# A grouped 3x3 convolution on one core: which images are computed by which of three schemes, and from where on a step is issued one image earlier

## The chip, the cores and the metric

The kernel runs on one core of a Trainium2 chip. The metric is the time of one execution on the device in microseconds; a kernel's time is the median of several executions. The engines are TensorE (PE, with its weight loads as PEld), VectorE (DVE), ScalarE (ACT), GpSimd (POOL) and SyncE (SP).

## What is computed

Input x has 160 images of 128 channels by 32x32 in float32. Each is normalised by groups of four channels (mean and variance over the group and all pixels), convolved 3x3 with padding 1, and the result is added to x. The weights come from U, five sets of 128x128x9, quantised in two steps. In memory the images of one set are five apart; the kernel takes all 32 images of set 0 first, then set 1, and so on.

```python
w = (v1 + v2).reshape(OUT_CH * N, IN_CH, K, K)          # v1, v2: U floored to steps s1, s2
act = conv_general_dilated(x.reshape(B // N, N * C, H, W), w, padding=1, feature_group_count=N)
x = x + act                                             # the convolution's input is _gn(x)
```

## The kernel before, in words

**Numbers.** The matmuls are in fp16. A normalised image is split into a high part hi (fp16 of it) and a low part lo (what is left, fp16 again), and both go through the convolution. An image's result lies in two PSUM banks, even and odd (of rows, or of columns), of 512 columns each.

**Two schemes.** The direct way to fill a bank is nine taps: one matmul for each of the nine weights, on the rows that this parity of output needs (`taps`, L771, matmul L784). The cheaper way goes through four combinations of neighbouring rows or columns with summed weights, three matmuls for each combination (`product`, L819, matmul L839). Combination 2 with the weights SUM is put into the even bank (`begin`, L847); a copy of that bank, half, is taken by ACT (`leave`, L902, copy L907); combination 3 with the weights DIFF goes on top (`complete`, L854); and DVE makes the odd bank as 2 x half - even (`odd_from_even`, L909, L914). Then the combinations 0 and 1 are added, one for each bank, in two passes (`main`, L892).

- A *by-rows* image uses taps for hi and combinations for lo. DVE makes lo (L747) and then the combinations, called rows, in three operations (L760, L768, L769). POOL makes the normalised z (L710), or ACT does for the first image of a statistics group (L636); ACT makes hi from it (L644).
- A *combined* image (`combined`, L647) uses combinations for both parts. The combinations v are made of the input itself: POOL makes part (L674, L704), DVE the rest (L686, L693). ACT scales them to vh (L734) and DVE makes vl (L740).
- Images 0 to 2 use taps for both parts (`direct_hi`, `direct_lo`).

Images 7 to 29 are combined where odd, 30 to 129 where i%5 is 0, 2 or 4, and the rest where i%4 is not 2.

**Order of work.** Each engine executes its queue in the order in which `run` (L993) issues it; nothing is reordered. Iteration i of its loop (L1125) issues `conv(i)` (L863) for PE, and around it the steps of images further on: the low part of image i+2 (i+3 after 13, both 15 and 16 at 13, by `step_of`, L983), the high part one further, v or z two further. On ACT an iteration has, in order: half, the sums over images to be measured (L241), the copies of the finished banks of image i-1 (L942), hi or vh, the squares of the images measured (L248), and columns of weights for the next set (`keep_taps`, L564). On DVE: the low part, the combine steps, odd of image i+1, then v (L686, L693), small statistics steps (L296 and following), and the measuring of a few images (L231, `BY_VECTOR`). Between them DVE gets one or two steps of the quantising of the next set's weights (`later.take`; L142 to L162). POOL's v, z and rstd wait for the last but one low-part instruction of DVE (L1207, `after`).

`conv(i)` has two forms. Before image `TWO_AHEAD` (28) it issues begin(i+1), main(i, 0), leave(i+1), complete(i+1), main(i, 1): half is awaited one pass later. From 28 on it issues complete(i+1), begin(i+2), main(i, 0), main(i, 1), and leave(i+2) follows among ACT's later steps, so half has a whole image's time.

**Buffers.** lo has four (image number modulo four), even four banks, odd three, rows and vl five together, hi and vh four each. POOL's accumulating DMA adds each result to an output that already holds the input (L963).

Of the kernel before, what the change touches and what calls it, by code (L numbers as in the profile page):

```python
# [36 lines left out]
class Later:  # L37
# [25 lines left out]
    def finish(self):  # L63
        run(self.steps)
# [110 lines left out]
def last_of(steps, last=None):  # L175
    for last in steps:
        pass
    return last


def run(steps):

    while True:
        try:
            next(steps)
        except StopIteration as end:
            return end.value
# [134 lines left out]
def general_path(tc, keep, steps, x, u, out):  # L322
# [8 lines left out]
    with tc.If(far > 0), ExitStack() as ctx:  # L331
# [9 lines left out]
        for n in range(N_SETS):  # L341
            un = one.tile([P, C, TAPS], F32, tag="u", name=f"g_u{n}")
            nc.sync.dma_start(un, uv[n])
            wn = one.tile([P, C, TAPS], F32, tag="w", name=f"g_w{n}")
            k1, k2 = run(steps.quantise(one, un, f"g{n}", F32))
            nc.vector.tensor_scalar_mul(wn, k1, steps.s1)
            nc.vector.scalar_tensor_tensor(wn, k2, steps.s2, wn, ALU.mult, ALU.add)
# [38 lines left out]
class Main:  # L386
# [23 lines left out]

    STAT_LEAD = 15
    FURTHER = 11
    TWO_AHEAD = 28
    LOAD_LEAD = 18
    CHUNKS = 11
    STEADY = 7
    BY_VECTOR = (8, 10, 11, 14, 19, 24, 29, 34)
    FIFTHS = 30
    THIRDS = 130
# [171 lines left out]
    def keep_sums(self, n, col):  # L591
        wt = self.wts[n, col]
        run(self.both_sums(
            self.nc.gpsimd, wt[:, self.SUM], wt[:, self.DIFF], *(wt[:, k] for k in range(ROW))
        ))
# [6 lines left out]
    def by_vector(self, i):  # L602
        return i in self.BY_VECTOR

# [42 lines left out]
    def combined(self, i):  # L647

        if i < self.STEADY or i >= self.imgs:
            return False  # L650

        if i < self.FIFTHS:
            return i % 2 == 1
        return i % 5 % 2 == 0 if i < self.THIRDS else i % 4 != 2

    def by_scalar_too(self, i):

# [113 lines left out]
    def taps(self, i, part, col, target, parities=(0, 1)):  # L771


        nc, H, W = self.nc, self.H, self.W
        tile, top = part
        n, _ = self.place(i)
        dw = col - 1
        c0, c1 = max(0, -dw), W - max(0, dw)
        for k in self.KS:
            for a in parities:  # L780

                first, end = int(a + k == 0), H // 2 - int(a + k == 3)
                s0 = 2 * first + a + k - 1 + top
                nc.tensor.matmul(  # L784
                    target[a][:, first:end, c0:c1],
                    self.wts[n, col][:, k, :],
                    tile[:, s0 : s0 + 2 * (end - first) - 1 : 2, c0 + dw : c1 + dw],
                    start=(i < self.FIRST and col == self.COLS[0] and k == 1 and top == 0),
                    stop=False,
                    skip_group_check=True,  # L790
                )
# [54 lines left out]

    def begin(self, i):  # L847

        even = self.bank_of(self.ps_even, i)
        self.eo[i] = [even]  # L850
        for step in self.KS:
            self.product(even, i, 2, step, self.SUM, start=step == self.KS[0])

    def complete(self, i):  # L854

        for step in self.KS:
            self.product(self.eo[i][0], i, 3, step, self.DIFF)

    def steady(self, i):

        return i >= self.TWO_AHEAD

    def conv(self, i, on_the_way):  # L863


        ahead = range(i + 1, self.imgs)[:1]
        if self.steady(i) and self.steady(i - 1):
            for k in ahead:
                self.complete(k)
            for k in range(i + 2, self.imgs)[:1]:  # L870
                self.begin(k)
            self.main(i, 0, lambda: on_the_way(self.COLS[1]))
            self.main(i, 1, lambda: on_the_way(self.COLS[2]))
        elif i == self.FIRST:
            self.main(i, 0)
            self.begin(i + 1)
            on_the_way(self.COLS[1])
            self.main(i, 1)
            on_the_way(self.COLS[2])
            self.leave(i + 1)  # L880
            self.complete(i + 1)
        else:
            self.begin(i + 1)
            self.main(i, 0, lambda: on_the_way(self.COLS[1]))
            self.leave(i + 1)
            self.complete(i + 1)
            if self.steady(i):
                self.begin(i + 2)
            self.main(i, 1, lambda: on_the_way(self.COLS[2]))
        del self.v[i]  # L890

    def main(self, i, a, between=lambda: None):  # L892

        to = self.eo[i][a]
        for step in self.KS:
            if step == self.KS[1] and a == 1 or step == self.KS[2] and a == 0:
                between()
            if not self.combined(i):
                self.taps(i, (self.hi[i], 0), step, self.eo[i], (a,))
            self.product(to, i, a, step, 2 * a)  # L900

    def leave(self, i):  # L902

        half = self.half[i] = self.evac.tile(
            [self.P, self.H // 2, self.W], F32, tag="half", name=f"half{i}"
        )
        self.nc.scalar.copy(half, self.eo[i][0])  # L907

    def odd_from_even(self, i):  # L909


        even, odd = self.eo[i][0], self.bank_of(self.ps_odd, i)
        self.eo[i].append(odd)
        self.nc.vector.scalar_tensor_tensor(  # L914
            odd, self.half.pop(i), 2.0, even, ALU.mult, ALU.subtract
        )
# [76 lines left out]
    def run(self):  # L993
# [54 lines left out]
        def measure(stage, *images):  # L1048
            for i in images:
                self.measure(i, (stage,))  # L1050
# [74 lines left out]
        for i in range(self.imgs):  # L1125
# [53 lines left out]
            if i < self.FIRST:  # L1179

                if i == 0:
                    measure(0, 8, 9, 10)
                if i == 1:
                    self.normalise(4)
                    self.high_part(4)
                if i == 2:
                    self.normalise(5)
                    measure(1, 9)
                    self.high_part(5)
                    self.odd_from_even(3)  # L1190
                    self.low_part(4)
                    run(self.combinations(4))
                    measure(0, 11)
                self.residual(j)
            else:

                last = None
                for k in self.step_of(i, 2):
                    if self.combined(k):
                        last = last_of(self.low_combined(k), last)  # L1200
                    else:
                        self.low_part(k)
                        later.take(1)
                        last = last_of(self.combinations(k), last)
                last = later.take(1, last)
                if last:
                    before = self.last_but_one(last)  # L1207
                    for st in scaled:
                        self.after(st.power(), before)
                    for k in self.step_of(i, 4):  # L1210
                        self.beside_pairs(k, before)
                if i > self.FIRST and self.by_hand(j):
                    self.residual(j)
                for k in by_scalar:
                    self.measure(k, (0,))
                if self.steady(i) and i + 2 < self.imgs:
                    self.leave(i + 2)
                if i > self.FIRST and not self.by_hand(j):
                    self.residual(j)
                    self.accumulate(j)  # L1220
                for st in ready:
                    if not st.late:
                        st.deviations()
                for k in self.step_of(i, 3):
                    if self.combined(k):
                        self.high_combined(k)
                        continue
                    if self.by_scalar_too(k):
                        self.normalise(k)
                    self.high_part(k)  # L1230
                for k in by_scalar:
                    self.measure(k, (1,))
# [95 lines left out]
```

## Time and profile before

| | us |
|---|---|
| median of 3 runs | 972.56 (971.38 to 973.38) |
| the profiled execution, its own time | 971.98 |
| its span, first to last instruction | 970.2 |
| mean granted TensorE clock | 0.993 of full |

The profile is of one execution. PE's busy time counts a matmul until its modelled end (0.37 to 0.38 us for 512 columns), while successive matmuls start 0.21 us apart, so a PE that is shown busy is one that never waits long. A bracket at the end of a timeline row gives the idle time of the engine ahead of it and what ended that. The granted clock is the share of full speed at which the array was let run.

| operation | engine, line | mean us |
|---|---|---|
| vl | DVE L740 | 2.50 |
| v, two parts | DVE L686, L693 | 1.66, 0.74 |
| lo; rows, three parts | DVE L747; L760, L768, L769 | 1.22; 0.69, 0.42, 0.42 |
| odd | DVE L914 | 0.69 |
| vh; hi; half | ACT L734; L644; L907 | 2.02; 1.07; 0.58 |
| z by POOL; by ACT | L710; L636 | 1.87; 1.27 |

### The profile page before, as it was taken

What the parts mean: (1) busy time and instruction counts of PE and PEld (TensorE: products, weight loads), DVE (VectorE), ACT (ScalarE), POOL (GpSimd) and SP (SyncE); (2) the same over time, 40 slices, a digit from 0 to 9 for tenths busy, and PEclk for the clock granted to TensorE, in tenths of its full rate; (3) what the DMA queues carried; (4) which work ended last, traced back from release to release, by engine and by line L of the source; (5) the groups of instructions that cost most, each with busy time, mean ns of one, the idle gap of its engine ahead of it and who ended that gap; (6) DMA issues with size and microseconds to landing.
All of it is one profiled execution on the core that took longest, in us unless ns stands there. A gap on an engine that the chain in (4) does not pass through costs nothing.

```text
span 970.2 us, 12948 instructions
## 1 busy us (share of the span) xinstructions
PE 928.3 (96%) x4432; PEld 434.6 (45%) x4432; DVE 858.9 (89%) x1125; ACT 863.3 (89%) x1320; POOL 446.0 (46%) x481
## 2 busy tenths in 40 slices
PE   2899979999999999999999999999999999999996
PEld 1444434444444444444444444444444444444442
DVE  7988878888899899998999899898989988889973
ACT  5779879998999999999999999999999999997660
POOL 4354433544453443454445444545444455454640
PEclk9999989999999999999999999999999999999998
DMA  9079999999999999999999999999999999756554
GB/s 353 29 270 351 329 353 330 328 326 329 321 314 317 259 283 294 276 284 269 290 252 308 286 282 284 289 277 297 263 274 266 290 280 258 162 90 102 95 93 128
DMA packets 67450, 254.23 MB, mean 262 GB/s; under 512 B 5296, under 2 KB 5296, under 8 KB 67376
## 3 DMA queue, kind: packets, MB, share of 16 engines
q1 hardware_dynamic: 45344, 173.09, 47.8%
q0 software_dynamic: 22032, 80.23, 44.1%
q8 instruction: 37, 0.61, 0.2%
q14 instruction: 37, 0.30, 0.1%
HBM read 89.19 MB, written 164.10 MB: 261 GB/s over the span
## 4 chain that ended last, share of the span: by engine, by line
PE 79%; ACT 10%; DVE 5%; issue 3%; DMA 2%; POOL 1%; SPq 0%; DVEq 0%; ACTq 0%; POOLq 0%
PE even L839 43%; PE odd L839 14%; PE even L784 11%; PE odd L784 11%; ACT junk L248 2%; ACT vh L734 2%; ACT sum L942 2%; ACT junk L241 2%; DMA u<-in_L_conv_U_dram 2%; ACT z L636 1%; ACT half L907 1%; ACT hi L644 1%; DVE ext L508 1%; DVE ext L509 1%; DVE lo L747 1%
## 5 line engine op out<-in xcount | busy, mean ns | idle before, releaser
L839 PEld LDWEIGHTS <-wt 128*128 128x128 f16 x1884 | 184.3, 99 | 211.2 <-issue 4.4
L740 DVE SCALAR_TENSOR_TENSOR vl<-v,rstd,vh 128x2048 f16<-128x2048 f32 x94 | 235.2, 2502 | 48.6 <-ACT vh L734 48.4
L839 PE MATMUL even<-vh,across 128*128 128x512 f16 x564 | 211.3, 375 | 3.5 <-ACT half L907 3.5
L839 PE MATMUL even<-vl,across 128*128 128x512 f16 x564 | 211.3, 375 | 1.7 <-DVE vl L740 1.7
L734 ACT ACTIVATE vh<-v,rstd 128x2048 f16<-128x2048 f32 x94 | 190.2, 2024 | 0.0
L784 PEld LDWEIGHTS <-wt 128*128 128x128 f16 x1242 | 121.7, 100 | 144.2 <-issue 6.6
L248 ACT ACTIVATE junk<-xt,mv 128x1024 uint8<-128x1024 f32 x152 | 176.4, 1160 | 0.3
L839 PE MATMUL even<-rows,wt 128*128 128x512 f16 x567 | 174.2, 381 | 2.5 <-ACT half L907 2.4
L963 POOL DMA_DIRECT2D out_dram<-sum x153 | 135.2, 884 | 89.7 <-ACT sum L942 74.5
L241 ACT ACTIVATE junk<-xt 128x1024 uint8<-128x1024 f32 x152 | 161.2, 1060 | 12.7 <-DMA xt<-in_x_dram 9.8
L839 PEld LDWEIGHTS <-across 128*128 128x128 f16 x1128 | 110.4, 98 | 135.5 <-issue 7.5
L784 PE MATMUL even<-hi,wt 128*128 128x496 f16 (+3 forms) x594 | 162.9, 379 | 4.8 <-DVE odd L914 3.8
L710 POOL TENSOR_SCALAR z<-xt,ngm,rstd 128x1024 f32<-128x1024 f32 x49 | 91.8, 1873 | 152.1 <-DVE rows L769 50.5
L784 PE MATMUL odd<-hi,wt 128*128 128x496 f16 (+3 forms) x594 | 161.0, 375 | 0.0
L686 DVE TENSOR_TENSOR v<-xt 128x960 f32<-128x960 f32 x94 | 155.8, 1658 | 0.5 <-POOL v L674 0.5
L907 ACT COPY half<-even 128x512 f32<-128x512 f32 x157 | 90.6, 577 | 60.1 <-PE even L839 57.1
L674 POOL TENSOR_SCALAR v<-xt,ngm 128x64 f32<-128x64 f32 x94 | 59.0, 628 | 172.8 <-DVE vl L740 74.8
L914 DVE SCALAR_TENSOR_TENSOR odd<-half,even 128x512 f32<-128x512 f32 x157 | 107.8, 687 | 17.3 <-PE even L839 13.8
L839 PE MATMUL even<-vh,wt 128*128 128x496 f16 (+1 forms) x282 | 105.6, 375 | 0.0
L839 PE MATMUL even<-vl,wt 128*128 128x496 f16 (+1 forms) x282 | 105.6, 375 | 0.0
L839 PE MATMUL odd<-vl,wt 128*128 128x496 f16 (+1 forms) x282 | 105.6, 374 | 0.0
L839 PE MATMUL odd<-vh,wt 128*128 128x496 f16 (+1 forms) x282 | 105.6, 374 | 0.0
(148 smaller groups left out, 1131.1 us busy)
## 6 DMA issues: line engine op xcount, KB each, us to landing
xt<-in_x_dram SPq DMA_DIRECT2D x78, 1024.0 KB, 9.6
out_dram<-sum POOLq DMA_DIRECT2D x153, 512.0 KB, 8.8
out_dram<-xt SPq DMA_DIRECT2D x76, 1024.0 KB, 14.2
out_dram<-xt SPq DMA_DIRECT2D x7, 512.0 KB, 6.1
u<-in_L_conv_U_dram SPq DMA_DIRECT2D x4, 576.0 KB, 14.7
xt<-in_x_dram SPq DMA_DIRECT2D x4, 512.0 KB, 9.8
range<-in_L_conv_U_dram SPq DMA_DIRECT2D x3, 576.0 KB, 8.0
u<-in_L_conv_U_dram SPq DMA_DIRECT2D x2, 288.0 KB, 3.0
```

What stands on the lines that cost most here:

```text
L241: self.nc.scalar.activation(junk, image, ACTF.Copy, scale=-1.0 / image.shape[1], accum_out=self.mv[:, j, 0:1],)
L248: self.nc.scalar.activation(junk, image, ACTF.Square, bias=self.mv[:, j, 0:1], accum_out=self.mv[:, j, 1:2],)
L674: return self.nc.gpsimd.tensor_scalar(self.view(self.v[i], 0, (512 + W // 2 - 1, 2), (W // 2, H)), self.view(self.image(i), 1, (W - 3, 2), ...
L686: nc.vector.tensor_tensor(self.view(v, 1, (511, 2), (half, H), (1, half - 1)), self.view(x, 1, (1, 2), (W, H), (2, half - 1)), self.view(x ...
L710: ins = nc.gpsimd.tensor_scalar(z, self.image(i), st.ngm[:, j], st.rstd[:, j], ALU.add, ALU.mult)
L734: self.nc.scalar.mul(vh, self.v[i], st.rstd[:, j])
L740: yield self.nc.vector.scalar_tensor_tensor(vl, self.v[i], st.rstd[:, j], self.hi[i], ALU.mult, ALU.subtract)
L784: nc.tensor.matmul(target[a][:, first:end, c0:c1], self.wts[n, col][:, k, :], tile[:, s0 : s0 + 2 * (end - first) - 1 : 2, c0 + dw : c1 + dw],
L839: self.nc.tensor.matmul(out, weights, moving, start=start and j == 0, stop=False, skip_group_check=True)
L907: self.nc.scalar.copy(half, self.eo[i][0])
L914: self.nc.vector.scalar_tensor_tensor(odd, self.half.pop(i), 2.0, even, ALU.mult, ALU.subtract)
L963: added = self.nc.gpsimd.dma_start(self.ov[n, :, b], self.sum.pop(i), accum_op=ALU.add)
```

## The change

Three things change.

1. `combined`: for images 30 to 129, three of five become five of eight (i*5%8 < 5), which makes 62 of 100 combined instead of 60, and other ones. All images that start a statistics group from 32 on are now combined.
2. Images 12 and 16, so far by rows, are *plain*: taps for lo as well as for hi, into both banks. They have no rows, no begin, half, complete or odd_from_even; `main` takes both banks when it starts its first pass.
3. `TWO_AHEAD` goes from 28 to 20: the second form of `conv` starts eight images earlier.

```diff
-    TWO_AHEAD = 28
+    TWO_AHEAD = 20
...
+    PLAIN = (12, 16)
...
-        return i % 5 % 2 == 0 if i < self.THIRDS else i % 4 != 2
+        return i * 5 % 8 < 5 if i < self.THIRDS else i % 4 != 2
+
+    def plain(self, i):
+        return i in self.PLAIN
...
-                    start=(i < self.FIRST and col == self.COLS[0] and k == 1 and top == 0),
+                    start=((i < self.FIRST or self.plain(i)) and col == self.COLS[0] and k == 1 and top == 0),
...
     def begin(self, i):
 
+        if self.plain(i):
+            return
...
     def complete(self, i):
 
+        if self.plain(i):
+            return
...
-        del self.v[i]
+        self.v.pop(i, None)
 
     def main(self, i, a, between=lambda: None):
 
+        if self.plain(i) and a == 0:
+            self.eo[i] = [self.bank_of(pool, i) for pool in (self.ps_even, self.ps_odd)]
         to = self.eo[i][a]
         for step in self.KS:
             if step == self.KS[1] and a == 1 or step == self.KS[2] and a == 0:
                 between()
             if not self.combined(i):
                 self.taps(i, (self.hi[i], 0), step, self.eo[i], (a,))
-            self.product(to, i, a, step, 2 * a)
+            if self.plain(i):
+                self.taps(i, (self.los[i % len(self.los)], 1), step, self.eo[i], (a,))
+            else:
+                self.product(to, i, a, step, 2 * a)
 
     def leave(self, i):
 
+        if self.plain(i):
+            return
...
     def odd_from_even(self, i):
 
 
+        if self.plain(i):
+            return
...
-                        last = last_of(self.combinations(k), last)
+                        if not self.plain(k):
+                            last = last_of(self.combinations(k), last)
```

## The prediction

> **What bounds the kernel now.** I first read the page's busy shares, then the table of windows, which shows by stage who is full, and then the timeline of the stage that isn't.
>
> ```profile
> span 970.2 us, 12948 instructions
> ...
> PE 928.3 (96%) x4432; PEld 434.6 (45%) x4432; DVE 858.9 (89%) x1125; ACT 863.3 (89%) x1320; POOL 446.0 (46%) x481
> ```
>
> The columns below are stage, its length, busy us of PE, PEld, DVE, ACT and POOL, then the granted clock.
>
> ```profile
> 95.00:130.00 35.00, 31.90 (x158) 15.17 (x156) 30.21 (x54) 32.34 (x50) 12.56 (x14) 1.00 1.04 339
> 130.00:145.00 15.00, 10.50 (x40) 4.28 (x39) 11.28 (x18) 8.76 (x14) 5.43 (x6) 0.77 1.04 357
> 145.00:175.00 30.00, 29.30 (x144) 13.84 (x142) 26.64 (x43) 28.35 (x46) 11.46 (x15) 1.00 1.04 329
> 175.00:250.00 75.00, 75.00 (x360) 34.98 (x358) 63.94 (x83) 68.73 (x109) 37.71 (x38) 1.00 1.04 327
> 250.00:800.00 550.00, 550.00 (x2645) 258.27 (x2643) 506.98 (x643) 534.53 (x823) 259.06 (x262) 1.00 1.01 284
> ```
>
> From 175 to 800 us PE never rests, at full clock; ACT is 97% and DVE 92% full behind it. There only fewer matmuls, or a new wait, can change the time. From 95 to 175 PE rests, and from 130 to 145 its clock is 0.77 on average. The half (L907) and odd (L914) rows come once per image from image 3 on, so they number the images: this is images 9 to 20. PE's rows there:
>
> ```profile
> 127.21 0.37 PE L839 MATMUL even<-vl,wt 128*128 128x496 f16 x1
> 128.86 0.81 PE L839 MATMUL even<-rows,wt 128*128 128x512 f16 x3 [1.28 <-ACT half L907]
> ...
> 130.91 0.38 PE L839 MATMUL even<-vh,across 128*128 128x512 f16 x1
> 132.99 0.38 PE L839 MATMUL even<-vl,across 128*128 128x512 f16 x1 [1.70 <-DVE vl L740]
> ...
> 133.83 0.37 PE L839 MATMUL even<-vl,across 128*128 128x496 f16 x1
> 137.00 0.99 PE L784 MATMUL even<-hi,wt 128*128 128x512 f16 x2 [2.79 <-DVE odd L914]
> ```
>
> Matmuls start 0.21 us apart at full clock, so start to start these stalls cost 1.65-0.21 = 1.44 (b: complete(14) waits for ACT's half of 14), 2.08-0.21 = 1.87 (c: begin(15) waits for vl of 15) and 3.17-0.21 = 2.96 (d: main(14) waits for odd of 14). Two more wait for half: (a) before 109.76, 2.0 us, complete(11), and (e) before 171.74, 0.86 us, complete(20). The windows 128.1:134.9 and 134.9:141.8 have clocks of 1.00 and 0.51: the clock halves right after the stalls. The even pass of image 14 then takes 137.00 to 141.88, 4.88 us; the same 12 matmuls of image 10 took 105.22 to 107.77, 2.55. So the slow clock costs 2.33 us.
>
> **The change, part by part.** *Matmuls.* A by-rows image has 30 (two passes of 9 taps and 3 products, and 3 each in begin and complete), a combined one 24, a plain one 36. Of images 30 to 129, 62 instead of 60 are combined: 12 matmuls fewer. The plain images add 6 each: 12 more, of the same shapes. A pass of 12 takes 2.55 us and three products 0.64 (128.86 to 129.50), so nine taps take 1.91 and a plain pass 3.82. A plain image thus costs 2x(3.82-2.55)-2x0.64 = +1.26 us, a swap from rows to combined as much less. Net: zero. PE gains only where it now rests.
>
> *Images 12 and 16 on DVE and ACT.* Each drops three row operations (L760, L768, L769; 109.72 less start 108.78 plus 0.33 to the next: 1.27 us in image 12), its odd (about 0.6) and its half, which moves ACT's next instruction from 115.22 to 114.75: 0.47. They do not all shift what follows. DVE after image 12 is held at 117.47 by POOL's rstd, which waits for a vl that is not earlier: DVE's gain there is lost. ACT has no gap from 109 to 134, so its 0.47 lives on until the half of 14.
>
> *Stall (b).* These ACT rows precede it:
>
> ```profile
> 126.72 1.15 ACT L248 ACTIVATE junk<-xt,mv 128x1024 uint8<-128x1024 f32 x1
> 127.77 0.19 ACT L248 ACTIVATION_READ_ACCUMULATOR junk<-xt,mv 128x1 f32 x1
> 127.86 0.47 ACT L564 ACTIVATE wt<-small 128x384 f16<-128x384 f32 x1
> 128.24 0.57 ACT L907 COPY half<-even 128x512 f32<-128x512 f32 x1
> ```
>
> The half now starts at 127.77 and ends at 128.34. PE, 1.26 later through image 12, wants to run complete(14) at 127.21+0.21+1.26 = 128.68. No wait is left: 1.44 gained, of which 1.26 pays for image 12.
>
> *Stalls (c) and (d).* DVE's rows:
>
> ```profile
> 128.37 0.16 DVE L296 TENSOR_SCALAR twice<-small 128x4 f32<-128x4 f32 x1 [1.26 <-ACT wt L564]
> ...
> 130.59 2.34 DVE L740 SCALAR_TENSOR_TENSOR vl<-v,rstd,vh 128x2048 f16<-128x2048 f32 x1
> 132.85 1.22 DVE L747 TENSOR_TENSOR lo<-z,hi 128x1024 f16<-128x1024 f32 x1
> 133.99 0.61 DVE L144 SCALAR_TENSOR_TENSOR tt<-tt,s1r,nnn 128x384 f32<-128x384 f32 x1
> 134.51 0.68 DVE L760 TENSOR_TENSOR rows<-lo 128x1024 f16<-128x1024 f16 x1
> ...
> 136.26 0.69 DVE L914 SCALAR_TENSOR_TENSOR odd<-half,even 128x512 f32<-128x512 f32 x1
> ```
>
> DVE waits here for ACT's L564, so it is 0.47 earlier too: vl of 15 lets PE go at 132.52. PE, 0.18 earlier than before at complete(14), stands there from 130.91-0.18+0.21 = 130.94: stall 1.58 instead of 1.87, 0.29 gained. Then the rows of 16 (134.51 to 135.79, 1.28) are gone from ahead of odd(14), and PE starts main(14) at 137.00-0.47-1.28 = 135.25 instead of 137.00. PE was free at 133.57; stall 1.68 instead of 2.96, 1.28 gained. Sum of (b) to (d): 3.0. What is late next is the same DVE chain, 1.7 us shorter.
>
> *The clock.* The window that preceded the drop, 128.1:134.9, had PE busy for 3.64 of 6.80 us; 107.6:114.5 with 5.08 of 6.90 lost nothing. With the new times PE rests 1.4 (131.1 to 132.5) and 1.5 us (133.7 to 135.2): in 128.1:134.9 it would be busy about 4.1 of 6.80. That lies between, and from 129 to 136 about 3.9 of 6.8, nearer the bad row. The gain is between 0 and 2.33. I take 2.33, because two short gaps in place of gaps of 1.3, 1.7 and 2.8 leave no stretch as empty as the one that was punished, but not by much.
>
> [...]
>
> *Stall (e).* Before image 20, ACT was idle 6.92 us waiting for half(16) (to 146.55), an instruction that goes; PE comes 2.8 us earlier after image 16 (1.75+2.33-1.26), so ACT has the room to follow. Stall (e) is of ACT's own making at image 18, where two images are measured and a z (L636) is ACT's: it keeps 0.4 to 0.9. I take 0.2 gained. Stall (a) lies ahead of every dropped instruction and stays.
>
> *A new wait.* The lo of 16 and of 20 goes into the buffer that the plain 12 and 16 read until their second pass ends. For 16 PE is long done. Image 16 ends on PE at 157.18-2.8 = 154.4, while DVE, at most 1.75+2.33 = 4.1 earlier, comes to the lo of 20 (before at 157.82) at 153.7 or later: up to 0.7 us of waiting. Behind it on DVE stand the rows of 20 and odd(18), before at 161.23, then done by 158.5; PE asks for it at about 162.3-2.8 = 159.5. Hidden; at most 0.7 if that cover is gone.
>
> *Two ahead from 20.* begin(i+2) comes one image sooner, so rows or vl must be there. The vl of 23 runs from 174.95 to 177.3. The odd of 21 waited for complete(21) until 179.16; a pass of 2.55, begin(22) and complete(22) later, at about 183, PE would ask for it. PE moves up by 2.8 at most, so some 3 us of cover stay. Were it gone, a stall like (e) would come once. In exchange half has an image's time instead of a pass. I count zero; bounds -0.3 to +1.
>
> *Images 30 to 129.* Two more combined images: ACT +2x(2.02-1.07) = 1.9 us (L734 for L644), DVE 2x(2.5+1.7+0.7-1.2-0.7-0.4-0.4) = +4.4 (the means of L740, L686, L693 less L747, L760, L768, L769). Groups starting at 48, 56, 88, 96 and 128 become combined, which takes five z of 1.27 from ACT: net -4.4. POOL gets about 9 us more, at 47%. DVE has 550-507 = 43 us of room: cover. Zero; bounds 0 to +2. Beyond 130 nothing moves.
>
> **Sum.** 3.0+2.33+0.2 = 5.5. The profiled execution took 971.98 us (970.2 and 1.8 around it), 0.6 under the median of 972.56. 971.98-5.5 = 966.5.
>
> **Rivals.** *The clock still halves*: gain 3.2, 968.8. For it: the nearness above. Against: less rest in all. *The stalls move on instead of going*: DVE behind 117.47 is held by POOL, and were L564 held too, only the 1.28 of (d) and about 0.2 remain, less 0.5 of new waits: 971.0; up to 2 more is within no change. Against: ACT's gapless rows. *Pairs stall PE (slower)*: combined pairs come twice in 8 images instead of once in 5, and where three follow each other (820, 843, 865 us) PE loses 0.76, 0.63, 0.76 to ACT's half. Were each of 12.5 periods to lose 0.72, +9.0, 971.98-5.5+9.0 = 975.5; it decides from 8 periods. Against: the 20 pairs of before lost 0.15 us twice (334 and 560 us), and ACT gets 4.4 us of room.
>
> **Chances.** Forecast 0.46 (965 to 968), clock still halved 0.26 (968 to 970), moved on 0.14 (970 to 973.5), pairs 0.14. 0.2% is 1.9 us, about what a measurement of this kernel can tell from no change. Faster 0.72, same 0.14, slower 0.14. With the unknowns (another 2 of (c) to (e) gone, or half of the third case) the range is 964.5 to 971.8.
>
> **What would show it.** Right: PE's row before complete(14) without a wait; odd(14) near 134.6; no window under clock 1.00 between 95 and 300; PE at 100% from 175 to 800. Wrong: waits on half or vl at images 21 to 28, or one per 8 images later; DVE's waits for vh longer than 22 us in 250:800.

## The result, and the profile after

The changed kernel takes 966.74 us (median of 5 executions, 965.43 to 967.71) against 971.38 of the kernel before in the same series (970.93 to 973.38): 0.9946 of it, with a 95% interval of 0.9932 to 0.9959, so 4.6 us less. The prediction was 966.5. The profiled execution took 967.71 us, with a span of 966.0. Lines are shifted by up to 17 in the changed kernel: L784 is now L788, L839 L843, L740 L744, L907 L922, L914 L931. Stalls (a) to (e) are those of the prediction.

The stages once more: length, busy us of PE, PEld, DVE, ACT, POOL, and the granted clock.

```profile
95.00:130.00 35.00, 33.18 (x164) 15.80 (x162) 28.79 (x50) 32.34 (x50) 12.63 (x14) 1.00 1.04 340
130.00:145.00 15.00, 11.89 (x45) 4.80 (x44) 10.77 (x16) 10.32 (x17) 5.55 (x6) 0.77 1.04 347
145.00:175.00 30.00, 29.73 (x146) 14.09 (x145) 25.27 (x40) 26.38 (x42) 11.44 (x15) 1.00 1.04 333
175.00:250.00 75.00, 75.00 (x360) 34.95 (x359) 66.46 (x87) 69.53 (x109) 38.14 (x39) 1.00 1.04 327
250.00:800.00 550.00, 550.00 (x2646) 258.49 (x2645) 515.02 (x634) 533.41 (x822) 264.07 (x269) 1.00 1.01 287
```

PE rests less from 95 to 175 and still never from there to 800, although DVE has 8 us more to do from 250 to 800 (515.02 for 506.98). But the clock of 130 to 145 is 0.77 as before: in this execution it halved again. PE's rows:

```profile
129.05 0.81 PE L843 MATMUL even<-rows,wt 128*128 128x512 f16 x3
...
131.10 0.38 PE L843 MATMUL even<-vh,across 128*128 128x512 f16 x1
132.94 0.38 PE L843 MATMUL even<-vl,across 128*128 128x512 f16 x1 [1.46 <-DVE vl L744]
...
133.78 0.37 PE L843 MATMUL even<-vl,across 128*128 128x496 f16 x1
135.81 1.41 PE L788 MATMUL even<-hi,wt 128*128 128x512 f16 x3 [1.65 <-DVE odd L931]
```

Complete(14), at 129.05, has no bracket any more: stall (b) is gone. Two rests stay, start to start less 0.21: 1.63 (c) and 1.82 (d). The three matmuls at 135.81 take 1.41 us instead of 0.80: half clock (0.50 granted from 134.70 to 141.52 us). ACT and DVE stand where they were foreseen, 0.42 later throughout, because this execution came 0.42 later to stall (a) (110.18 for 109.76):

```profile
127.82 0.47 ACT L565 ACTIVATE wt<-small 128x384 f16<-128x384 f32 x1
128.19 0.57 ACT L922 COPY half<-even 128x512 f32<-128x512 f32 x1
```

```profile
128.86 1.28 DVE L231 BATCH_NORM_STATS2 st<-xt 128x6 f32<-128x512 f32 x2
...
130.55 2.34 DVE L744 SCALAR_TENSOR_TENSOR vl<-v,rstd,vh 128x2048 f16<-128x2048 f32 x1
132.81 1.22 DVE L751 TENSOR_TENSOR lo<-z,hi 128x1024 f16<-128x1024 f32 x1
133.94 0.61 DVE L144 SCALAR_TENSOR_TENSOR tt<-tt,s1r,nnn 128x384 f32<-128x384 f32 x1
134.59 0.56 DVE L145 TENSOR_TENSOR lt<-tt,nnn 128x384 f16<-128x384 f32 x1
135.07 0.69 DVE L931 SCALAR_TENSOR_TENSOR odd<-half,even 128x512 f32<-128x512 f32 x1
```

The three row operations of image 16, which stood between L144 and L145, are gone, and odd(14) starts at 135.07 instead of 136.26.

**A way to take an execution apart.** Single executions of one kernel differ by 2 to 3 us, as much as some of the effects. Three things do it, and the trace separates them: the *start* (up to the matmul that ends stall (a): 109.6 to 111.2 us), the *stretch* from there to the start of the last matmul, and the *end* (7.2 to 8.8 us). The start is 109.6 to 110.3 where the clock holds, and 110.7 to 111.2 in the six profiles where it fell for 3.41 us at 40 to 41 us. In the stretch I add up what PE's rows lose: rests over 0.24 us (start to start less 0.21; in the row "none plain" also one of 0.18 at 131 us), and what matmuls at half clock take longer. What is left is PE's own work.

| profile | stretch | rests 110 to 175 | half clock | rests 175 to 805 | left |
|---|---|---|---|---|---|
| before | 851.79 | 7.13 | 2.42 | 0 | 842.24 |
| before, second profile | 852.20 | 7.13 | 2.81 | 0 | 842.26 |
| changed | 848.62 | 3.89 | 2.89 | 0 | 841.84 |
| changed, second profile | 847.49 | 3.87 | 1.66 | 0 | 841.96 |
| two ahead alone | 851.20 | 7.16 | 1.71 | 0 | 842.33 |
| five of eight alone | 849.24 | 7.14 | 2.74 | 0 | 839.36 |
| plain images alone | 848.60 | 3.88 | 0 | 0 | 844.72 |
| 12 alone plain | 848.99 | 5.48 | 2.91 | 0 | 840.60 |
| 16 alone plain | 849.19 | 5.58 | 2.95 | 0 | 840.66 |
| zero matmuls in the rests | 845.81 | 1.08 | 0 | 0 | 844.73 |
| image 24 later | 844.15 | 2.18 | 0 | 0 | 841.97 |
| image 24 later, none plain | 845.14 | 5.63 | 0 | 0 | 839.51 |
| two of three combined | 842.98 | 2.20 | 0 | 4.95 | 835.83 |
| three of four from 98 | 849.59 | 2.21 | 0 | 10.47 | 836.91 |

The last column moves with the number of matmuls: 12 fewer give 842.24-839.36 = 2.9, 12 more 2.5, 30 fewer 6.1, 24 fewer 5.1. The rests of 110 to 175 repeat to 0.03 us wherever the program there is the same.

### The profile page after: what moved, and what is told of

Its sections match the earlier page's. It is cut to its first block, busy times and chain, and to the rows that moved or that the text cites. A ratio compares the mean times of both kernels' runs of the same rounds, so it can differ in the third digit from the quotient of the medians.

```text
span 966.0 us, 12938 instructions
## 1 busy us (share of the span) xinstructions
PE 928.2 (96%) x4432; PEld 434.4 (45%) x4432; DVE 865.0 (90%) x1110; ACT 859.5 (89%) x1313; POOL 446.5 (46%) x488
## 4 chain that ended last, share of the span: by engine, by line
PE 81%; ACT 8%; DVE 5%; issue 2%; DMA 2%; POOL 1%; SPq 0%; DVEq 0%; ACTq 0%; POOLq 0%
PE even L843 44%; PE odd L843 15%; PE even L788 11%; PE odd L788 11%; ACT vh L738 2%; ACT junk L248 2%; DMA out_dram<-xt 1%; ACT sum L959 1%; ACT junk L241 1%; DMA range<-in_L_conv_U_dram 1%; DVE lo L751 1%; ACT z L637 1%; ACT hi L645 1%; DVE v L690 0%; ACT half L922 0%
## 5 line engine op out<-in xcount | busy, mean ns | idle before, releaser
L843 PEld LDWEIGHTS <-wt 128*128 128x128 f16 x1860 | 181.9, 99 | 207.3 <-issue 2.6
L744 DVE SCALAR_TENSOR_TENSOR vl<-v,rstd,vh 128x2048 f16<-128x2048 f32 x96 | 238.4, 2484 | 38.6 <-ACT vh L738 38.5
L843 PE MATMUL even<-vh,across 128*128 128x496 f16 (+1 forms) x576 | 216.1, 375 | 3.5 <-ACT half L922 3.5
L843 PE MATMUL even<-vl,across 128*128 128x496 f16 (+1 forms) x576 | 215.9, 375 | 1.5 <-DVE vl L744 1.5
L738 ACT ACTIVATE vh<-v,rstd 128x2048 f16<-128x2048 f32 x96 | 194.1, 2022 | 0.0
L788 PEld LDWEIGHTS <-wt 128*128 128x128 f16 x1242 | 121.7, 100 | 142.3 <-issue 5.8
L843 PEld LDWEIGHTS <-across 128*128 128x128 f16 x1152 | 112.8, 98 | 138.1 <-issue 7.4
L690 DVE TENSOR_TENSOR v<-xt 128x960 f32<-128x960 f32 x96 | 164.6, 1715 | 0.5 <-POOL v L678 0.5
L843 PE MATMUL even<-rows,wt 128*128 128x512 f16 x531 | 163.1, 381 | 0.8 <-ACT half L922 0.7
L788 PE MATMUL even<-hi,wt 128*128 128x496 f16 (+3 forms) x576 | 158.1, 379 | 3.4 <-DVE odd L931 2.7
L788 PE MATMUL odd<-hi,wt 128*128 128x496 f16 (+3 forms) x576 | 156.3, 375 | 0.0
L714 POOL TENSOR_SCALAR z<-xt,ngm,rstd 128x1024 f32<-128x1024 f32 x52 | 82.3, 1582 | 158.0 <-DVE vl L744 75.4
L678 POOL TENSOR_SCALAR v<-xt,ngm 128x64 f32<-128x64 f32 x96 | 69.9, 728 | 163.5 <-DVE vl L744 88.4
L922 ACT COPY half<-even 128x512 f32<-128x512 f32 x155 | 89.2, 575 | 57.0 <-PE even L843 53.9
L931 DVE SCALAR_TENSOR_TENSOR odd<-half,even 128x512 f32<-128x512 f32 x155 | 106.3, 686 | 15.5 <-PE even L843 11.2
L843 PE MATMUL even<-vh,wt 128*128 128x496 f16 (+1 forms) x288 | 107.9, 375 | 0.0
L843 PE MATMUL even<-vl,wt 128*128 128x496 f16 (+1 forms) x288 | 107.9, 375 | 0.0
L843 PE MATMUL odd<-vl,wt 128*128 128x496 f16 (+1 forms) x288 | 107.8, 374 | 0.0
L843 PE MATMUL odd<-vh,wt 128*128 128x496 f16 (+1 forms) x288 | 107.8, 374 | 0.0
```

The lines of the kernel that those rows point to most:

```text
L678: return self.nc.gpsimd.tensor_scalar(self.view(self.v[i], 0, (512 + W // 2 - 1, 2), (W // 2, H)), self.view(self.image(i), 1, (W - 3, 2), ...
L690: nc.vector.tensor_tensor(self.view(v, 1, (511, 2), (half, H), (1, half - 1)), self.view(x, 1, (1, 2), (W, H), (2, half - 1)), self.view(x ...
L714: ins = nc.gpsimd.tensor_scalar(z, self.image(i), st.ngm[:, j], st.rstd[:, j], ALU.add, ALU.mult)
L738: self.nc.scalar.mul(vh, self.v[i], st.rstd[:, j])
L744: yield self.nc.vector.scalar_tensor_tensor(vl, self.v[i], st.rstd[:, j], self.hi[i], ALU.mult, ALU.subtract)
L788: nc.tensor.matmul(target[a][:, first:end, c0:c1], self.wts[n, col][:, k, :], tile[:, s0 : s0 + 2 * (end - first) - 1 : 2, c0 + dw : c1 + dw],
```

## The experiments

Times below are medians; each ratio is to the kernel before on the same chip in the same series.

**The changed kernel again.**

> The changed kernel once more. My theory: about 4.6 us under the kernel before (1.44+0.24+1.14 of stalls (b), (c), (d), 0.4 of (e), the rest from executions in which the clock does not halve between 130 and 142 us and from the end). Of its executions some are 2.3 us shorter, with a mean clock near 0.998 instead of 0.995 to 0.996. Rival: the profiled pair differed by chance in its end, and the gain is only about 3 us.

967.3 us, 0.9948 (0.9936 to 0.9961). Of the ten executions of the changed kernel, two have a mean clock of 0.998 (965.43 and 964.84 us), the others 0.995 or 0.996 (966.64 to 967.88, mean 967.15): 2.0 us apart, where 2.3 was expected. An execution's mean clock also counts the drop at 40 us, where there is one, and the half clock behind the last matmul (1.85 us of the span in the first profile of the changed kernel, 5.83 in that of the kernel before). A value of 0.998 leaves no room for 3.41 us of half clock beside 1.85; 0.995 doesn't say where the clock fell, which only a profile shows. The gain of 4.6 to 4.7 us by the medians repeats.

**The kernel before again**, for a second profile.

> The kernel before once more, for a second profile. Between the first pair of profiles the stretch from stall (a) to the last matmul shrank by 3.2 us and the end behind the last matmul by 1.5 (8.66 to 7.18). My theory: the stretch is again 851 to 852 us with rests of 7.1 us between 110 and 175, and the end is chance between executions: 7.2 to 8.8. Rival (the end belongs to the kernel): again 8.6 to 8.8.

972.82 us. The stretch and its rests repeat (852.20 and 7.13). The end is 8.12 us, under the 8.6 to 8.8 that the rival asked for and within the 7.2 to 8.8 of my theory.

**The parts alone.** Only the plain images:

```diff
-    TWO_AHEAD = 20
+    TWO_AHEAD = 28
...
-        return i * 5 % 8 < 5 if i < self.THIRDS else i % 4 != 2
+        return i % 5 % 2 == 0 if i < self.THIRDS else i % 4 != 2
```

> Only images 12 and 16 are made plain; 28 and three of five stay. My theory: PE has 12 matmuls more (+2.5 us), the stalls (b), (c), (d) shrink as in the changed kernel (-2.9) and (e) a little: the time is 0 to 1 us under the kernel before, 2.3 less where the clock stays up. Rival (the gain is all from the new pattern in images 30 to 129 and from ACT's five z that go): 2.5 us slower than before.

969.45 us, 0.9979 (0.9969 to 0.9989): 2.0 us faster by the ratio, more than the 0 to 1 expected, since by their mean clock half of the executions had no drop: five of ten at 0.998 (mean 968.45), five at 0.995 (970.94). The stretch shows +2.5 of work and -3.25 of rests.

Only the switch at 20 (`TWO_AHEAD = 20` in the kernel before):

> Only the switch at image 20 instead of 28. My theory: no wait stands at images 20 to 28 in either form, so the time is that of before within 0.5 us. Rival (two ahead takes slack from the low parts, which the plain images give back): a new wait of 0.5 to 1 us at images 21 to 24. Other rival (two ahead removes the wait at 171 us): 0.9 faster.

971.28 us, 0.9998 (0.9989 to 1.0007). No new wait, and the rest at 171 us is the same 0.86: it does nothing that can be measured.

Only five of eight:

```diff
-        return i % 5 % 2 == 0 if i < self.THIRDS else i % 4 != 2
+        return i * 5 % 8 < 5 if i < self.THIRDS else i % 4 != 2
```

> Only five of eight instead of three of five in images 30 to 129: 12 matmuls fewer. My theory: PE is full there before and after, so 12 x 0.21 = 2.5 us faster, all stalls ahead of 172 us unchanged. Rival (pairs of combined images make PE wait for ACT's half, as at 820 to 865 us): waits of 0.7 us once in eight images, up to 9 us, so 6 slower.

968.28 us, 0.9964 (0.9951 to 0.9976): 3.5 us faster, where 2.5 (0.9974) was expected and lies within the interval. From 175 to 805 us no row of PE waits, so pairs stall nothing; two short waits of before (0.15 each) are gone. The rival that would have made the change slower falls here.

**Each plain image alone** (`PLAIN = (12,)` and `PLAIN = (16,)` in the changed kernel).

> The changed kernel with 12 alone plain, 16 by rows again. My theory: PE has 6 matmuls less (-1.26), stall (d) grows from 1.82 to 2.97 (+1.15) and (e) back to 0.86 (+0.4): the same time as the changed kernel within 0.5 us where the clock does the same, and some 0.5 more for falling more often: 967 to 968. Rival (the plain images are what the gain comes from): 2 us or more slower than the changed kernel.

> The changed kernel with 16 alone plain, 12 by rows again. My theory: 6 matmuls less (-1.26), stall (b) is back (+1.44), (c) back to 1.87 (+0.24), (d) as changed: 0.4 slower than the changed kernel where the clock does the same, 967 to 968. Rival (plain 12 helps nothing but (b) and costs as much): within 0.3 of the changed kernel; other rival (12 carries the gain): 2 us slower.

968.58 us, 0.9963 (0.9949 to 0.9976), and 966.84 us, 0.9949 (0.9936 to 0.9963). PE's waits from 115 to 175 us, first with 12 alone plain, then with 16 alone (total, times, longest):

```profile
PE even L788 <- DVE odd L931: 2.8, 1, 2.8
PE even L843 <- DVE vl L744: 1.5, 1, 1.5
PE even L843 <- ACT half L922: 0.7, 1, 0.7
```

```profile
PE even L843 <- DVE vl L744: 1.7, 1, 1.7
PE even L788 <- DVE odd L931: 1.7, 1, 1.7
PE even L843 <- ACT half L922: 1.6, 2, 1.3
```

Image 12 removes the wait of 1.3 for half(14), image 16 takes 1.1 off the wait for odd(14). Each costs 1.26 us of matmuls. A plain image thus buys hardly more than it costs. The medians, 0.1 and 1.8 us above the changed kernel's, say little beside the clock's 2.3. The profiles say more, as all three have a drop of 6.83 us: the stretch is 848.99 and 849.19 us, against 848.62 with both plain, so one plain image less costs 0.4 to 0.6, which speaks against the rival that either of them carries the gain.

**What halves the clock.** 13 matmuls with a matrix of zeros fill the two rests:

```diff
+            if i == 14:
+                self.fill(i - 1, 6)
             self.begin(i + 1)
+            if i == 14:
+                self.fill(i - 1, 7)
             self.main(i, 0, lambda: on_the_way(self.COLS[1]))
...
+    def fill(self, i, count):
+        moving = self.los[3].rearrange("p h w -> p (h w)")[:, :512]
+        for _ in range(count):
+            self.nc.tensor.matmul(
+                self.eo[i][1].rearrange("p r w -> p (r w)"), self.zero, moving,
+                start=False, stop=False, skip_group_check=True,
+            )
...
```

> The changed kernel with 13 matmuls by a matrix of zeros, 6 ahead of begin(15) and 7 behind it, added to the finished odd bank of image 13: 1.28 and 1.49 us of work inside the two rests of 1.63 and 1.82 us that are left. The results stay the same. My theory (the rests are what halves the clock): no execution halves its clock between 130 and 145 us, all are like the drop-free ones of the changed kernel, about 965.0, so 2 us under the changed kernel's median. Rival (the drop hangs on something else, or empty matmuls do not count): some executions still fall to half, median 967. Rival (the matmuls get in the way): waits for odd and vl unchanged but begin(15) or main(14) later, 967 to 969.

964.91 us, 0.9931 (0.9917 to 0.9945). PE's rows, with the filling at L908:

```profile
131.02 1.46 PE L908 MATMUL odd<-lo,zero 128*128 128x512 f16 x6
132.32 0.38 PE L843 MATMUL even<-vh,across 128*128 128x512 f16 x1
132.87 0.38 PE L843 MATMUL even<-vl,across 128*128 128x512 f16 x1 [0.17 <-DVE vl L744]
...
133.92 1.67 PE L908 MATMUL odd<-lo,zero 128*128 128x512 f16 x7
135.73 0.79 PE L788 MATMUL even<-hi,wt 128*128 128x512 f16 x3
```

And the window from 130 to 145 us, with the granted clock of 1.00:

```profile
130.00:145.00 15.00, 14.69 (x70) 6.70 (x70) 13.55 (x19) 12.83 (x20) 6.42 (x7) 1.00 1.04 347
```

Main(14) starts when it started before, since odd(14) has not moved, but its three matmuls take 0.79 us, not 1.41. By the medians, matmuls that add nothing make the kernel 1.8 us faster (1.5 by the ratios). In the profiles the stretch is 2.81 us shorter: the filling costs as much work (2.89) as it takes from the rests (2.81), and the 2.89 of half clock are gone. My theory holds: the profile has no drop, and all five executions (964.40 to 966.07) lie below the eight of the changed kernel whose mean clock was 0.995 or 0.996. One of the five, 966.07 at 0.997, may have had a drop somewhere; it has no profile. The rival that they get in the way falls.

**What the rests are made of.** DVE measures image 24 an iteration later:

```diff
+            if i == 13:
+                measure(0, 24)
             if i >= self.FIRST:
-                measure(0, *by_vector)
+                measure(0, *[k for k in by_vector if k != 24])
```

> The changed kernel, but DVE measures image 24 one iteration later (1.69 us of work that stands just ahead of vl of 15), behind odd of 14. My theory (the rests at 131 and 134 us are DVE's chain from the small statistics steps over vl, lo of 16 and odd of 14): vl of 15 ends 1.7 us earlier, the first rest goes from 1.63 to about 0, the second stays near 1.8, and the clock falls less often: 1.7 to 3.5 us under the changed kernel, about 964. Rival (another wait stands right behind, for vh of 15 or the z of 18): the second rest grows by what the first loses, and the time stays at 967.

963.72 us, 0.9916 (0.9903 to 0.993), 3.0 us under the changed kernel. DVE's and PE's rows:

```profile
128.57 0.16 DVE L302 TENSOR_TENSOR dv<-dv,mv 128x4 f32<-128x4 f32 x1
128.66 2.34 DVE L744 SCALAR_TENSOR_TENSOR vl<-v,rstd,vh 128x2048 f16<-128x2048 f32 x1
...
133.18 0.69 DVE L931 SCALAR_TENSOR_TENSOR odd<-half,even 128x512 f32<-128x512 f32 x1
133.77 1.28 DVE L231 BATCH_NORM_STATS2 st<-xt 128x6 f32<-128x512 f32 x2
```

```profile
130.89 0.38 PE L843 MATMUL even<-vh,across 128*128 128x512 f16 x1
131.11 0.38 PE L843 MATMUL even<-vl,across 128*128 128x512 f16 x1
...
131.95 0.37 PE L843 MATMUL even<-vl,across 128*128 128x496 f16 x1
133.92 0.80 PE L788 MATMUL even<-hi,wt 128*128 128x512 f16 x3 [1.59 <-DVE odd L931]
```

The first rest is gone and the second is 1.76, as expected: the whole chain moved up, and the measuring (L231) stands behind odd(14), where DVE used to wait 4.09 us for PE. With one rest left the clock holds in the profile:

```profile
130.00:145.00 15.00, 13.41 (x66) 6.17 (x65) 14.51 (x22) 13.26 (x20) 6.41 (x7) 1.00 1.04 347
```

The same without plain images (`PLAIN = ()`):

> Image 24 measured later, five of eight and two ahead from 20, but no plain image. My theory, against the version with both: PE 12 matmuls less (-2.5), (b) back (+1.44), first rest +0.2, (d) +1.15, (e) +0.43: 0.7 slower, and the clock falls in some executions again, so 964.5 to 966. Rival (with DVE's chain 1.7 us shorter the plain images are not needed any more): 1 to 2.5 faster.

965.73 us, 0.9935 (0.9921 to 0.9948): 2.0 slower than with them, within the range I gave but more than the 0.7 of the stalls. The profile has rests of 5.63 us instead of 2.18, among them two new ones for odd at 147 and 159 us (0.58, 0.46) in place of (e), and 2.5 less work: +1.0 in the sum. The other 1.0 us I can only ascribe to start and end (0.3 and 0.95 longer in the profiles), which one profile each doesn't prove.

**How far the pattern goes.** On top of image 24 later, two of three combined (`return i % 3 != 1 if i < self.THIRDS`), and three of four from image 98 (`THIRDS = 98`):

> Image 24 later, and in images 30 to 129 two of three combined instead of five of eight: 67 instead of 62. PE has 30 matmuls less, -6.3 us. ACT gets 5 x 0.96 and four z of 1.26 more, 9.8 us, where it has rested 16.6 of 550 us in the changed kernel's profile, and the span it has shrinks by 6.3. My theory (PE alone bounds that stretch as long as ACT has any rest): 3 to 6 us under the version with five of eight, with first waits for ACT's half or vh. Rival (pairs without a pause between them are what breaks it): waits of 0.7 us per pair, 10 us slower.

> Image 24 later, and the pattern of three combined in a row (three of four) from image 98 instead of 130: 66 instead of 62 combined, PE 24 matmuls less, -5.0 us. Each run of three makes PE wait 0.63 to 0.81 us for ACT's half from 812 us on. My theory (each run of three costs that, with the measuring still on ACT): 8 runs x 0.73 = +5.8, so 0.8 slower than with five of eight. Rival (PE alone bounds): 5 faster.

962.76 us, 0.9899 (0.9883 to 0.9914), and 968.81 us, 0.9967 (0.9954 to 0.9979). The first is the fastest version here, 4 us under the changed kernel, but only 1.0 under five of eight (1.7 by the ratios, as the two ran on different chips), where I expected 3 to 6; the second is 5.1 slower than five of eight, where I expected 0.8. The busy us from 250 to 800 and PE's waits from 175 to 805, for two of three:

```profile
250.00:800.00 550.00, 546.38 (x2621) 255.90 (x2620) 522.50 (x639) 542.34 (x827) 269.50 (x268) 1.00 1.02 289
```

```profile
PE even L843 <- ACT half L922: 2.3, 4, 0.7
PE even L843 <- DVE vl L744: 1.1, 4, 0.4
```

and PE's waits for three of four from 98:

```profile
PE even L843 <- DVE vl L744: 5.6, 5, 1.6
PE even L843 <- ACT half L922: 3.1, 6, 0.7
```

Two of three: 6.1 us less work, 4.95 lost to rests, 2.9 of it for ACT's half and 2.0 for DVE's vl. ACT is 98.6% full (542.34 of 550) and DVE 95% (522.50). I had taken PE alone to bound this part as long as ACT rests at all; PE begins to wait while ACT still rests 1.4% of the time. Three of four: the waits for half came nearly as priced (six rests of 0.62 to 0.83 us), but I had left out DVE: five rests for vl, 0.57 to 1.74 us. Neither theory had that. What makes vl late isn't shown. Ahead of the first of these (the vl that starts at 673.39 us) DVE's rows since the vl before hold 1.95 us of quantising, and 1.58 us in which DVE waited for ACT and POOL; no run here takes either away.

## Why the prediction was right, and where it was wrong

The median fits to 0.2 us and the direction is right, but not every term held, and the close fit is partly luck. The forecast was a gain of 5.5 us; by the medians it was 4.6. The forecast counted from 971.98, which is 0.6 above the 971.38 of this series, and that made up for most of the 0.9. In the profiled pair the clock's 2.33 didn't come, and 1.48 us of the end, which no term had, stood in for part of it.

- *Matmuls, net zero*: right. The last column of the table is 842.2 before and 841.9 changed; alone, the plain images cost 2.5 and five of eight saves 2.9 (2.5 of matmuls, 0.3 of short waits).
- *Stall (b) gone, ACT 0.47 earlier*: right. The half starts at 128.19, which is 127.77 and the 0.42 by which this execution is later.
- *Stalls (c) and (d)*: foreseen 1.58 and 1.68, measured 1.63 and 1.82. In (d), 0.13 is L145: it starts 0.65 us after L144 (134.59 after 133.94), behind L144's end, where the first of the rows started 0.52 after it.
- *Stall (e)*: 0.44 left, as the lower bound had it; 0.43 gained instead of 0.2. All rests: 7.13-3.89 = 3.24 us less; 3.2 were foreseen.
- *The clock, 2.33 gained*: the step that failed. In the profiled execution the clock fell for 6.83 us as before and cost 2.89 instead of 2.42 us: 0.47 lost. By the sign that I had set, no window under clock 1.00 between 95 and 300 us, this term was wrong. I judged by stretches of 6.8 us, as long as the drop itself. Here are stretches half as long, three of the changed kernel, bounded by the drop, and two of the plain images alone, whose profile has no drop:

```profile
127.90:131.30 3.40, 3.40 (x19) 1.69 (x17) 2.87 (x11) 3.40 (x8) 0.00 (x0) 1.00 1.04 363
131.30:134.70 3.40, 1.40 (x6) 0.48 (x5) 3.37 (x4) 3.07 (x6) 0.00 (x0) 1.00 1.04 312
134.70:138.10 3.40, 2.29 (x6) 0.84 (x6) 3.40 (x3) 3.40 (x7) 2.30 (x2) 0.50 1.03 423
```

```profile
130.50:133.90 3.40, 1.93 (x10) 0.77 (x8) 3.40 (x4) 3.24 (x5) 0.00 (x0) 1.00 1.04 281
133.90:137.30 3.40, 1.75 (x9) 0.77 (x8) 3.37 (x5) 3.23 (x6) 2.30 (x2) 1.00 1.01 414
```

  Behind the 3.40 us in which PE was busy for 1.40 the granted clock is 0.50. In the other profile the same two rests fall on two stretches, with 1.93 and 1.75, and the clock stayed at 1.00. Stretches laid elsewhere would divide those rests otherwise, so why it held there isn't shown. Of the three profiles with these two rests, two have a drop (2.89 and 1.66 us of half clock in the table) and one has none, and I had made it a yes or no.
- *What stood in its place*: in the profiled pair, 971.98 to 967.71 is 4.27 us. The stretch gave 3.17 (3.24 of rests and 0.40 of work, less 0.47 of clock), the end 1.48, the later start took 0.42. The rival "the clock still halves" describes this execution: 3.2 for the stretch. What takes the medians from there to 4.6 isn't shown, since only profiled executions can be taken apart; the execution without a drop (965.43) and the end, which I hadn't foreseen, both point that way. I can't show that the change shortened the end: it is 8.66 and 8.12 us in two profiles of the kernel before, 7.18 and 7.17 in two of the changed one, but 7.55 with five of eight alone and 8.57 with image 24 later and none plain. In the first pair the issue of the last two stores takes SP 2.12 us, then 0.81 (but 0.81 too with the plain images alone, whose end is 7.97):

```profile
962.41 2.12 SPq L952 DMA_DIRECT2D out_dram<-xt  x2
```

```profile
959.66 0.81 SPq L969 DMA_DIRECT2D out_dram<-xt  x2
```

- *New wait for the buffer of lo*: DVE waited 0.86 us before lo of 20 (0.7 foreseen), hidden as said.
- *Two ahead*: zero, as counted. *Images 30 to 129*: no new wait, and DVE's waits for vh fell from 22.3 to 18.8 us. The loads were mis-sized: from 250 to 800 us DVE got 8.0 us more (4.4 foreseen), ACT 1.1 less (4.4 foreseen) and POOL 5.0 more (9). It cost nothing, because PE stayed full.
- *The rivals*: pairs stall nothing. "The stalls move on" is wrong, because ACT has no gap in which its 0.47 could be lost.

By the ratios the parts alone give 2.0, 0.2 and 3.5 us, 5.7 in sum, and together 5.1 to 5.2: nearly additive. Most of it is five of eight, work taken off a PE that is full; the plain images repay their own 2.5 us with 3.25 of rests, and the rest is clock.

## What to carry to other kernels

Where an engine is full, count its work; where it rests, follow the one chain that ends last, instruction by instruction, and ask whether what is removed lies on it. Here moving 1.7 us of DVE's measuring off that chain was worth more than making two images plain. A short rest of PE can cost more than itself through the clock (with the rest of 1.63 us the 2.89 of half clock went too), so look at the granted clock behind every group of rests; and before a difference of 2 us is believed, take executions apart into start, stretch, end and clock.

## What the runs showed of the hardware

In the first profile of the kernel before, the granted clock is 0.50 from 134.94 to 141.77 us and 1.00 from there to 964.38; in that of the changed kernel it is 0.50 from 134.70 to 141.52 and 1.00 from there to 964.13. Each of these drops lasts 6.83 us. With two ahead alone, it is 0.50 from 137.40 to 140.80 (1.71 us of half clock in the table). In the 3.4 us ahead PE was busy for 1.21 us before (131.53 to 134.94), 1.42 in the changed kernel (131.28 to 134.69) and 0.60 with two ahead alone (134.00 to 137.40). At stall (a) it was busy for 1.58 and 1.59 of 3.41 us in the first pair (107.63 to 111.04, 107.39 to 110.80), and the clock stayed at 1.00 until the drop.

With rests of 1.44, 1.87 and 2.96 us, all four profiles show a drop (2.42, 2.81, 1.71 and 2.74 us of half clock in the table); with 12 or 16 alone plain, the one profile of each (2.91, 2.95); with 1.63 and 1.82, two of three (2.89, 1.66 and 0); with a single rest of 1.76, none of three. With image 24 later and none plain, a rest of 2.97 stands some 6 us behind one of 1.44, and no drop followed in the one profile. So two rests of 1.63 and 1.82 us, with 1.05 us of matmuls between them, were enough to halve the clock in two of three profiles.
